# A sparse graph network on one core: the neighbour lists' numbers on ACT instead of GpSimd, and DVE's constants first

## The chip, the core and the metric

The kernel runs on one core of a Trainium2 chip. A core has five engines that run their own instruction streams and wait for each other through semaphores: PE (matrix multiply; PEld is its weight load), DVE (vector), ACT (activations), POOL (GpSimd) and SP, which here only issues DMAs. Sixteen DMA engines move data between HBM and the on-chip memory SBUF; PSUM holds matmul results. The metric is the time of one execution on the device in microseconds (us). Before the change the median of three runs is 1838.98 us (1837.8 to 1839.6).

## The reference: what is computed

Four graph layers over n = 4096 nodes with 256 features. Each normalises x, applies relu, and adds an attention over the neighbours that `adj` names; `adj` is a 4096 x 4096 matrix of int32, symmetric, with ones on the diagonal, and very sparse (about 0.2% ones).

```python
adj = bernoulli(0.000976562); adj = (adj | adj.T | eye).astype(int32)
h = max(layernorm(x), 0); x = x + L0(h, adj)   # four heads, leaky relu, softmax over neighbours, elu
h = max(layernorm(x), 0); x = x + L1(h, adj)   # one head, adds h @ W as well
h = max(layernorm(x), 0); x = x + L2(adj, h)   # four heads with biases
h = max(layernorm(x), 0); x = x + L3(h, adj)   # q, k, v attention, masked by adj.T
# L0, per head:
Wh = (h @ W);  e_ij = leaky_relu(s_i + s_j, 0.2) where adj_ij else -inf
out = elu(softmax_j(e) @ Wh)
```

## The kernel before, in words

A row below means 128 nodes, one to a partition; there are `nt` = 32 of them. The kernel has two parts. The **scan** (`scan`, 0 to about 430 us) reads the 64 MB of `adj` once and turns each node's row of it into a list of at most 24 neighbour numbers. The **layers** (`layers`) then never touch `adj`: for each place of the lists they gather neighbours' table rows with indirect DMAs from POOL (line 755) and weigh them. A dense version exists for inputs that the lists cannot hold; it does not run on these inputs.

*One row in the scan.* SP loads a row of `adj` in four quarters (`load`, L250, eight buffers); ACT casts each quarter to fp8 (`cast`, L261). In `marks`, PE makes from 512 columns a PSUM tile in which a neighbour stands as MARK plus its distance from the end (L476 with `mark`, L481 with the constants `stands` and `places`), and DVE takes the largest 8 of each 256 columns (MAX8, L483). After eight such steps `merge` picks the row's largest 24 into `s_top` (L491, L493). `number` turns these into table indices in `self.ids`, a part of the tile `s_keep`: POOL clips them to [MARK, MARK + n] (L500) and writes MARK + n minus that as uint32 (L503). An empty place becomes n, the number of a filler row.

*Layer 0 starts inside the scan.* During the first 36 steps `table` makes layer 0's table (ACT L325, L336, L341; PE L333, L748), which SP stores to HBM (L384). `early(j)` then serves rows 2j and 2j + 1: POOL fetches the table rows of six neighbours each, 12 indirect DMAs (L755, tile `s_g`, three buffers), DVE, ACT, PE and again ACT weigh and sum them (L523 to L560). `sort` ranks all nodes by their number of neighbours; its result `s_pos` (L639) says where each node goes. `to_place(t)` sends row t there with an indirect DMA from POOL (L645, `s_placed`). When all 32 sends have landed, `reload` reads the rows back in their new order and the layers begin.

*What sets the order.* PE, DVE, ACT and SP run in program order. The program is written as a loop over steps: `at` counts them, four to half a row (`t = at // 4`, `halves` = 64), so row r is marked in steps 8r to 8r + 7 and merged in the last of these. `plan` puts further work of an engine at a step, and at each step ACT's comes first, then PE's, the marks, the merge, DVE's and POOL's, and last the sends. POOL is not in the list of hand-ordered engines: its order is chosen by the framework's scheduler from when it takes things to be ready; only numbers and fetches keep their order among themselves (`in_turn`), and a send stays behind the last fetch written before it. In the kernel before, the number of row r is planned on POOL at 8(r + 1). A pair j has its fetches at `begin` = max(4(10 + j), 4(4j + 4)); its first DVE work stands at `last`, which is at least 17 steps later and 13 after the pair before; its ACT copy comes 20 steps after `last`. Sends are allowed from t = 59 on, except at t = 60 and t = 64, at most 12 of them before t = 64:

```python
if t > halves - 6 and t not in (halves - 4, halves):
    upto = min(placed + (2 if s % 2 else 1), 12 if t < halves else nt)
```

*The start.* SP brings x in eight groups of four rows (`bring`, L272). Before the loop, DVE computes statistics of groups 0, 1 and 2 (L569, L570), ACT and DVE make their scales (`norms_of`, L575 to L585), and DVE sums layer 0's weights (L166, L169). DVE's part of the constants (`constants`, L424 to L453) comes after group 0 and the weights. The class defines `constants` twice; the later definition is the one that is called, so the first hunk of the diff below is in a function that never runs.

Of the kernel before, what the change touches and what calls it, by code (L numbers as in the profile page):

```python
# [9 lines left out]
F32 = mybir.dt.float32  # L10
# [3 lines left out]
AF = mybir.ActivationFunctionType  # L14
ALU = mybir.AluOpType
# [4 lines left out]
P = 128  # L20
# [17 lines left out]
TOPK = 24  # L38
# [6 lines left out]
MARK = 8192.0  # L45
# [24 lines left out]
class Sparse:  # L70
# [30 lines left out]
    def constants(self):  # L101
        nc, const = self.nc, self.const
        self.ident = const.tile([P, P], F32, name="s_ident")
        make_identity(nc, self.ident)
        self.ident_bf = const.tile([P, P], BF16, name="s_ident_bf")
        nc.vector.tensor_copy(self.ident_bf, self.ident)
        self.mark = const.tile([P, P], BF16, name="s_mark")
        nc.vector.tensor_scalar(self.mark, self.ident, MARK, None, ALU.mult)

        self.below = const.tile([P, P], BF16, name="s_below")  # L110
        ones = self.ones = const.tile([P, P], BF16, name="s_ones")
        nc.vector.memset(ones, 1.0)
        nc.vector.memset(self.below, -1.0)
        nc.gpsimd.affine_select(
            out=self.below, in_=self.below, pattern=[[-1, P]], compare_op=ALU.is_ge, fill=0.0,
            base=0, channel_multiplier=1,
        )
        self.eps = const.tile([P, 1], F32, name="s_eps")
        nc.vector.memset(self.eps, EPS)

    def load_w(self, name, w):
        w_sb = self.const.tile([P, KC, D], F32, name=f"s_w_{name}")
        if len(w.shape) == 3:
            for c in range(KC):
                self.nc.sync.dma_start(
                    out=w_sb[:, c, :].rearrange("p (h f) -> p h f", h=4),
                    in_=w[:, ts(c, P), :].rearrange("h p f -> p h f"),
                )
        else:
            self.nc.sync.dma_start(out=w_sb, in_=w.rearrange("(c p) f -> p c f", p=P))  # L130
        return w_sb
# [105 lines left out]
    def scan(self, w0, a0):  # L237
# [3 lines left out]
        nc, nt, n = self.nc, self.nt, self.n  # L241
        halves, groups = 2 * nt, nt // 4
# [3 lines left out]
        def load(upto):  # L246
            while state["load"] < min(upto, 4 * nt):
                q = state["load"]
                raw[q] = self.pool.tile([P, n // 4], I32, name=f"s_raw_{q}", tag="raw", bufs=RAW)
                nc.sync.dma_start(  # L250
                    out=raw[q], in_=self.adj[ts(q // 4, P), ts(q % 4, n // 4)]
                )
                state["load"] += 1

        def cast(upto):
            while state["cast"] < min(upto, 4 * nt):
                q = state["cast"]
                r, h = divmod(q, 4)
                if h == 0:
                    low[r] = self.pool.tile([P, n], F8, name=f"s_low_{r}", tag="low", bufs=5)  # L260
                nc.scalar.activation(  # L261
                    low[r][:, ts(h, n // 4)], raw.pop(q), AF.Copy, saturate=False,
                    accum_out=self.sums[:, r, h : h + 1],
                )
                state["cast"] += 1
# [2 lines left out]
        make_identity(nc, self.ident)  # L268
        self.eps = self.const.tile([P, 1], F32, name="s_eps")
        nc.vector.memset(self.eps, EPS)  # L270
        xl = lambda g: self.keep[:, 4 * g : 4 * (g + 1), 0:D]
        bring = lambda g: nc.sync.dma_start(  # L272
            out=xl(g),
# [2 lines left out]
        norms, scale = {}, {}  # L276

        def stats(g, k):
            if k == 0:
                norms[g] = self.norms_of(self.pool, xl(g), 4, f"t{g}")  # L280
            next(norms[g])

        def scaled(g):
            scale[g] = next(norms[g])

        bring(0)
        first = self.extended("l0", w0, a0, 4)
# [3 lines left out]
        bring(1)  # L291
        load(RAW - 2)
        bring(2)
        for k in range(4):
            stats(0, k)
        next(norms[0])
        scaled(0)
        *_, (self.we0, _) = first
        cast(2)
        self.constants()  # L300
        for g in range(1, 3):
            for k in range(4):
                stats(g, k)
            next(norms[g])
            scaled(g)
            cast(2 * g + 2)
        later = self.weights()
        next(later)

# [2 lines left out]
        def plan(engine, at, *work):  # L312
            todo[engine].setdefault(at, []).extend(work)

        def run(engine, at):
            for work in todo[engine].pop(at, ()):
                work()
# [31 lines left out]
        for g in range(3, groups):  # L349
            begin = 4 * (g - 3)  # L350
# [2 lines left out]
            plan("act", begin + 6, lambda g=g: next(norms[g]))  # L353
            plan("dve", begin + 8, lambda g=g: scaled(g))
        for r in range(nt):
            plan("pool", 8 * (r + 1), lambda r=r: self.number(r))
        whole, last = [], 0
        for j in range(nt // 2):
            begin = max(4 * (10 + j), 4 * (4 * j + 4))
            stages = self.early(j)  # L360
            step = lambda stages=stages: next(stages)
            plan("pool", begin, step)

            last = max(last + 13 if j else begin + 24, begin + 17)
            plan("dve", last, step)
            for k in range(3):
                plan("dve", last + 2 + k, step)
            for k in range(EARLY + 1):
                plan("pe", last + 6 + 2 * k, step)
            plan("act", last + 2 * EARLY + 8, step)  # L370
            whole.append(last + 2 * EARLY + 8)
# [6 lines left out]
        for at in range(end + 1):  # L378
            t, s = divmod(at, 4)
            r, half = divmod(t, 2)  # L380
            if s == 0:
                g = t - 3
                if 0 <= g < groups:
                    nc.sync.dma_start(  # L384
                        out=self.tab[0][4 * g * P : 4 * (g + 1) * P, :].rearrange(
                            "(t p) w -> p t w", p=P
                        ),
                        in_=self.keep[:, 4 * g : 4 * (g + 1), D : D + W],
                    )
                if t + 3 < groups:  # L390
                    bring(t + 3)
                if 2 <= t < 7:
                    next(later, None)
            if s in (0, 2):
                load(state["cast"] + RAW)
                cast(2 * t + 4 + min(10, max(0, t - 8)) + s // 2 + 1)
            run("act", at)
            run("pe", at)
            if t < halves:
                if s == 0 and half == 0:  # L400
                    cand = self.pool.tile(
                        [P, n // CH, 8], F32, name=f"s_cand_{r}", tag="cand", bufs=2
                    )
                self.marks(r, 4 * half + s, low[r], cand)
                if s == 3 and half == 1:
                    self.merge(r, cand)
            run("dve", at)
            run("pool", at)
            if t > halves - 6 and t not in (halves - 4, halves):

                upto = min(placed + (2 if s % 2 else 1), 12 if t < halves else nt)
                while placed < upto and whole[placed // 2] < at:
                    self.to_place(placed)
                    placed += 1
# [80 lines left out]
    def number(self, r):  # L495

        nc, n = self.nc, self.n
        ids = self.pool.tile([P, TOPK - 1], F32, name=f"s_ids_{r}", tag="ids")
        self.in_turn(
            nc.gpsimd.tensor_scalar(ids, self.top[:, r, 1:], MARK, MARK + n, ALU.max, ALU.min)  # L500
        )
        self.in_turn(
            nc.gpsimd.tensor_scalar(  # L503
                self.ids[:, r, 0 : TOPK - 1], ids, -1.0, MARK + n, ALU.mult, ALU.add
            )
        )

    def early(self, j):
# [1167 lines left out]
```

## Time and profile before

| | |
|---|---|
| median of 3 runs | 1838.98 us (1837.8 to 1839.6) |
| the profiled execution | 1841.32 us |
| its span, first to last instruction | 1839.6 us |
| granted PE clock, mean | 0.751 |
| DVE busy | 1379.9 us, 75% |
| POOL busy | 1184.8 us, 64% |
| PE busy | 994.8 us, 54% |
| ACT busy | 423.7 us, 23% |
| number, L500 and L503 | 32 of each on POOL, median 298 and 229 ns |
| fetch or send on POOL, L755 and L645 | about 0.95 and 0.97 us each, 0.30 between two |
| last merge of the scan ends | 380.76 us |
| last send of the scan ends | 427.77 us |
| first fetch of the layers | 432.29 us |

A timeline line gives the start, the duration, the engine, the line of the kernel, the operation, the tiles that it writes and reads, and in brackets how long the engine was idle before it and what ended that. A count (x4) means that several instructions are merged. A share of busy time is a mean over stages with different limits, so each stage has to be read by itself.

### The profile page before, as it was taken

The numbers are of one execution on the slowest core, as the hardware profiler recorded it, in microseconds if no ns is written. First come the engines' busy times: TensorE is split into PE (matmuls) and PEld (weight loads), VectorE is DVE, ScalarE is ACT, GpSimd is POOL, SyncE is SP. The second block draws the span as 40 slices with busy tenths as digits, with TensorE's granted clock in tenths as the row PEclk, the third lists the DMA queues.
The fourth block names the chain that finished last, engine by engine and source line by source line (L and its number), as shares of the span: only waits on it lengthen the run. The fifth ranks groups of instructions, "written<-read, shape, count | busy, mean of one in ns | idle before, by whom it ended". The sixth has DMA issues, their size and how long they took to land. (4 is left out here: it accounts for less than half of the span.)

```text
span 1839.6 us, 14362 instructions
## 1 busy us (share of the span) xinstructions
PE 994.8 (54%) x2569; PEld 481.7 (26%) x2569; DVE 1379.9 (75%) x3900; ACT 423.7 (23%) x1240; POOL 1184.8 (64%) x1324
## 2 busy tenths in 40 slices
PE   4878787750666611222232167788785344565555
PEld 3523232220455400111111023343342111221122
DVE  6899989850688808888888257888885587887777
ACT  5864435000244401111111002222222000000000
POOL 1067756676566357777776477777772577776774
PEclk9988889875788855555555588889987676777777
DMA  9899877348533134444444344444443577666763
GB/s 319 281 394 363 287 259 254 97 148 242 168 87 88 51 84 128 131 132 130 132 132 121 69 111 133 134 135 131 136 131 97 156 215 210 208 208 181 209 205 108
DMA packets 123017, 312.89 MB, mean 170 GB/s; under 512 B 31236, under 2 KB 49671, under 8 KB 122920
## 3 DMA queue, kind: packets, MB, share of 16 engines
q0 software_dynamic: 68064, 207.46, 39.7%
q1 hardware_dynamic: 54856, 104.44, 16.2%
q14 instruction: 73, 0.60, 0.1%
q8 instruction: 24, 0.39, 0.1%
HBM read 276.80 MB, written 35.00 MB: 169 GB/s over the span
## 5 line engine op out<-in xcount | busy, mean ns | idle before, releaser
L755 POOL DMA_INDIRECT s_ring<-s_tab,s_near x924 | 883.8, 956 | 356.7 <-issue 190.4
L1033 PE MATMUL s_acc<-s_ring,s_ident 128*128 128x512 f32 x588 | 319.5, 697 | 183.3 <-issue 95.0
L1033 PEld LDWEIGHTS s_acc<-s_ring,s_ident 128*128 128x128 f32 x588 | 130.5, 228 | 368.2 <-issue 245.5
L755 POOL DMA_INDIRECT s_g<-s_tab,s_keep x192 | 183.2, 954 | 64.3 <-issue 57.0
L483 DVE MAX8 s_cand<-s_pt 128x8 f32<-128x256 f32 x512 | 181.6, 417 | 16.4 <-PE s_pt L481 15.9
L1028 DVE TENSOR_TENSOR s_ring<-s_ring,s_shares 128x2048 f32<-128x2048 f32 (+7 forms) x121 | 187.5, 1573 | 0.0
L740 PE MATMUL s_pht<-s_ident,s_h 128*128 128x128 f32 x128 | 34.3, 361 | 248.0 <-ACT s_h L732 248.0
L748 PE MATMUL s_ps<-s_we_l,s_ht 128*128 128x264 f32 x256 | 113.4, 586 | 79.2 <-ACT s_ht L742 79.2
L999 DVE SCALAR_TENSOR_TENSOR s_acc<-s_ring,s_p,s_acc 128x256 f32<-128x256 f32 x277 | 135.7, 490 | 9.7
L261 ACT ACTIVATE s_low<-s_raw 128x1024 fp8e4<-128x1024 int32 x128 | 134.2, 1050 | 21.3 <-DMA s_raw<-in_adj_dram 18.1
L556 PE MATMUL s_ae<-s_g,s_ident 128*128 128x512 f32 x192 | 113.7, 688 | 36.5 <-DVE s_g L547 36.5
L913 DVE TENSOR_TENSOR s_e<-s_ring,s_rx 128x8 f32<-128x8 f32 (+12 forms) x87 | 15.7, 181 | 148.0 <-DMA s_ring<-s_tab,s_near 143.0
L476 PE MATMUL s_pt<-s_low,s_mark 128*128 128x512 fp8e4 x256 | 107.7, 421 | 34.3 <-DVE s_cand L483 15.0
L748 PE MATMUL s_ps_kv<-s_wkv,s_ht 128*128 128x512 f32 x128 | 82.9, 782 | 73.6 <-ACT s_ht L742 73.6
L932 DVE TENSOR_TENSOR s_ring<-s_ring,s_shares 128x2048 f32<-128x2048 f32 (+7 forms) x48 | 81.1, 1690 | 47.8 <-DMA s_ring<-s_tab,s_near 31.5
L481 PE MATMUL s_pt<-s_places,s_stands 128*128 128x512 bf16 x256 | 106.5, 416 | 1.4 <-DVE s_stands L453 1.4
L952 ACT ACTIVATE s_shares<-s_e 128x32 f32<-128x32 f32 (+8 forms) x87 | 17.4, 200 | 387.8 <-DVE s_e L945 340.2
L575 ACT ACTIVATE s_y<-s_mv,s_eps 128x1 f32<-128x1 f32 x96 | 28.3, 294 | 294.0 <-DVE s_mv L570 294.0
L740 PEld LDWEIGHTS s_pht<-s_ident,s_h 128*128 128x128 f32 x128 | 18.3, 172 | 287.9 <-ACT s_h L732 271.9
L748 PEld LDWEIGHTS s_ps<-s_we_l,s_ht 128*128 128x128 f32 x256 | 63.0, 272 | 110.0 <-ACT s_ht L742 100.1
L935 DVE TENSOR_REDUCE s_e<-s_ring 128x32 f32<-128x2048 f32 (+7 forms) x48 | 81.2, 1692 | 1.7
L1021 PE MATMUL s_acc<-s_me,s_ident 128*128 128x512 f32 x60 | 42.8, 803 | 70.8 <-DVE s_me L1014 67.2
(193 smaller groups left out, 1673.4 us busy)
## 6 DMA issues: line engine op xcount, KB each, us to landing
s_raw<-in_adj_dram SPq DMA_DIRECT2D x128, 512.0 KB, 7.8
s_ring<-s_tab,s_near POOLq DMA_INDIRECT x924, 3.0
s_rx<-s_placed SPq DMA_DIRECT2D x32, 262.0 KB, 8.0
s_tab<-s_kv SPq DMA_DIRECT2D x32, 256.0 KB, 2.8
s_tab<-s_keep SPq DMA_DIRECT2D x8, 528.0 KB, 6.8
s_tab<-s_rx SPq DMA_DIRECT2D x32, 132.0 KB, 2.3
s_keep<-in_x_dram SPq DMA_DIRECT2D x8, 512.0 KB, 4.1
s_vself<-s_tab SPq DMA_DIRECT2D x32, 128.0 KB, 2.9
```

Of the source, the lines that this page charges most:

```text
L261: nc.scalar.activation(low[r][:, ts(h, n // 4)], raw.pop(q), AF.Copy, saturate=False, accum_out=self.sums[:, r, h : h + 1],)
L476: nc.tensor.matmul(pt, lhsT=self.mark, rhs=lo[:, ts(g, IB)], start=True, stop=False)
L481: nc.tensor.matmul(pt, lhsT=self.stands[:, g, :], rhs=self.places, start=False, stop=True)
L483: nc.vector.max(out=cand[:, g * (IB // CH) + k, :], in_=pt[:, ts(k, CH)])
L556: nc.tensor.matmul(acc, lhsT=self.ident, rhs=g[:, :, k, 0:D], start=False, stop=(k == E - 1))
L748: self.nc.tensor.matmul(ps[:, :width], lhsT=ht[:, c, :], rhs=w[:, c, :], start=(c == 0), stop=(c == KC - 1),)
L755: return self.nc.gpsimd.indirect_dma_start(out=out, out_offset=None, in_=table[:, :], in_offset=bass.IndirectOffsetOnAxis(ap=idx, axis=0),)
L932: nc.vector.tensor_tensor(kq, kq, q.unsqueeze(1).to_broadcast([P, m, D]), ALU.mult)
L935: nc.vector.tensor_reduce(e[:, k0 : k0 + m, :], kq.rearrange("p k (h d) -> p k h d", h=4), AX.X, ALU.add)
L999: nc.vector.scalar_tensor_tensor(acc, g[:, k, 0:D], p[:, k, :], acc, ALU.mult, ALU.add)
L1028: nc.vector.tensor_tensor(v, v, p[:, k0 : k0 + m, :].unsqueeze(3).to_broadcast([P, m, H, D // H]), ALU.mult)
L1033: nc.tensor.matmul(both, lhsT=self.ident, rhs=g[:, k : k + 2, v0 : v0 + D], start=(k == 0 and not full), stop=(k + 2 >= K),)
```

## The change

Four edits:

- `number` runs on ACT: two Relu activations, each with a bias per partition. The first takes MARK away (negative results become 0), the second computes relu(n - a). The values are the same as before. It is planned at step 8(r + 1) + 2 on ACT instead of 8(r + 1) on POOL. The two biases are new constants, filled by DVE memsets.
- `begin` of a pair's fetches is 16(j + 1) + 3 instead of 16(j + 1) where this term is the larger; its later stages follow.
- Sends are held back in the four steps from 256 on only; those of t = 60 are no longer held.
- At the start `self.constants()` comes ahead of all statistics; group 0 joins the loop of the other two.

```diff
@@ scan
+        self.over = self.const.tile([P, 1], F32, name="s_over_mark")
+        nc.vector.memset(self.over, -MARK)
+        self.none = self.const.tile([P, 1], F32, name="s_none_n")
+        nc.vector.memset(self.none, float(n))
...
-        for k in range(4):
-            stats(0, k)
-        next(norms[0])
-        scaled(0)
-        *_, (self.we0, _) = first
-        cast(2)
         self.constants()
-        for g in range(1, 3):
+        for g in range(3):
             for k in range(4):
                 stats(g, k)
             next(norms[g])
             scaled(g)
             cast(2 * g + 2)
+            if g == 0:
+                *_, (self.we0, _) = first
...
-            plan("pool", 8 * (r + 1), lambda r=r: self.number(r))
+            plan("act", 8 * (r + 1) + 2, lambda r=r: self.number(r))
...
-            begin = max(4 * (10 + j), 4 * (4 * j + 4))
+            begin = max(4 * (10 + j), 16 * (j + 1) + 3)
...
-            if t > halves - 6 and t not in (halves - 4, halves):
+            if t > halves - 6 and not nt // 2 * 16 <= at < nt // 2 * 16 + 4:
@@ number
-        ids = self.pool.tile([P, TOPK - 1], F32, name=f"s_ids_{r}", tag="ids")
-        self.in_turn(
-            nc.gpsimd.tensor_scalar(ids, self.top[:, r, 1:], MARK, MARK + n, ALU.max, ALU.min)
-        )
-        self.in_turn(
-            nc.gpsimd.tensor_scalar(
-                self.ids[:, r, 0 : TOPK - 1], ids, -1.0, MARK + n, ALU.mult, ALU.add
-            )
+        a = self.pool.tile([P, TOPK - 1], F32, name=f"s_ids_{r}", tag="ids")
+        nc.scalar.activation(a, self.top[:, r, 1:], AF.Relu, bias=self.over)
+        nc.scalar.activation(
+            self.ids[:, r, 0 : TOPK - 1], a, AF.Relu, bias=self.none, scale=-1.0
         )
```

The first hunk of the full diff adds the same two tiles to the unused definition of `constants`.

More of the change, by code (lines that the diff above doesn't have):

```diff
@@ L270, in scan @@
         nc.vector.memset(self.eps, EPS)
+        self.over = self.const.tile([P, 1], F32, name="s_over_mark")
+        nc.vector.memset(self.over, -MARK)
+        self.none = self.const.tile([P, 1], F32, name="s_none_n")
+        nc.vector.memset(self.none, float(n))
         xl = lambda g: self.keep[:, 4 * g : 4 * (g + 1), 0:D]
```

## The prediction

> **What bounds the kernel now.** First the clock and span of the one core (1839.6 us, clock 0.751), then the windows of the scan and the hand-over to the layers, because every edit lies before 430 us. The page's chain of work that ended last accounts for some 1% of the span, so I follow the end of the scan by hand. The windows (window, its length, then busy us and instructions of PE, PEld, DVE, ACT, POOL; clock; DMA share; GB/s):
>
> ```profile
> 50.00:100.00 50.00, 43.42 (x200) 26.38 (x199) 45.12 (x160) 44.50 (x99) 5.37 (x11) 0.97 0.90 290
> 300.00:350.00 50.00, 34.16 (x101) 13.38 (x102) 44.65 (x119) 13.40 (x28) 31.22 (x39) 0.85 0.48 158
> 350.00:400.00 50.00, 33.01 (x88) 12.32 (x86) 34.98 (x101) 1.47 (x4) 35.48 (x43) 0.84 0.38 125
> 400.00:450.00 50.00, 9.37 (x14) 3.49 (x14) 8.79 (x21) 1.32 (x3) 35.04 (x37) 0.57 0.71 233
> ```
>
> DVE sets the pace of the scan (45 of 50 us), with ACT as full beside it only up to 100 us, where it also makes layer 0's table. From 350 on DVE empties and POOL does not: its 35 us are descriptors at 0.95 us, each followed by 0.30 us that the trace calls issue, so it is full. The timeline of POOL and DVE there (start, us, engine, line, [idle before]):
>
> ```profile
> 361.66 0.30 POOL L500 TENSOR_SCALAR s_ids<-s_top 128x23 f32<-128x23 f32 x1 [2.35 <-DVE s_top L491]
> ...
> 376.66 0.95 POOL L755 DMA_INDIRECT s_g<-s_tab,s_keep  x1 [0.30 <-issue]
> 377.91 0.99 POOL L645 DMA_INDIRECT s_placed<-s_keep,s_pos  x1 [0.30 <-issue]
> ...
> 380.47 0.29 DVE L491 MAX8 s_top<-s_cand 128x8 f32<-128x128 f32 x1
> ...
> 384.28 0.96 POOL L645 DMA_INDIRECT s_placed<-s_keep,s_pos  x1 [0.30 <-issue]
> 385.28 0.34 POOL L500 TENSOR_SCALAR s_ids<-s_top 128x23 f32<-128x23 f32 x1
> 385.69 0.23 POOL L503 TENSOR_SCALAR s_keep<-s_ids 128x23 uint32<-128x23 f32 x1
> 385.90 0.29 POOL L500 TENSOR_SCALAR s_ids<-s_top 128x23 f32<-128x23 f32 x1
> 386.27 0.23 POOL L503 TENSOR_SCALAR s_keep<-s_ids 128x23 uint32<-128x23 f32 x1
> 386.99 1.08 POOL L755 DMA_INDIRECT s_g<-s_tab,s_keep  x1 [0.49 <-issue]
> ...
> 426.80 0.97 POOL L645 DMA_INDIRECT s_placed<-s_keep,s_pos  x1 [0.30 <-issue]
> 430.36 0.16 POOL L711 IOTA s_place_of<- 128x32 f32 x1 [2.59 <-DMA s_placed<-s_keep,s_pos]
> ```
>
> The last row's list is ready on DVE at 380.76, but its fetches begin at 386.99: POOL is sending six rows away (377.91 to 385.24), then makes four number instructions. After 386.99 it goes without a gap through 12 fetches and 20 sends to 427.77; the layers' first fetch follows at 432.29. So the end of this stage is the start of the last 12 fetches plus 40.8 us.
>
> At the start DVE waits for x and then for ACT:
>
> ```profile
> 14.54 0.61 PE L481 MATMUL s_pt<-s_places,s_stands 128*128 128x512 bf16 x1 [1.39 <-DVE s_stands L453]
> 15.65 0.43 DVE L569 BATCH_NORM_STATS2 s_st_t<-s_keep 128x6 f32<-128x256 f32 x1 [1.16 <-DMA s_keep<-in_x_dram]
> 27.91 0.16 DVE L582 SCALAR_TENSOR_TENSOR s_rn_t<-s_y_t 128x4 f32<-128x4 f32 x1 [5.05 <-ACT s_h_t L325]
> ```
>
> **What the Trainium skill says.** "ScalarE: Activation LUTs", section "Table sets: the hidden batching unit", says that relu is in every table set. The trace agrees: one table load in the whole scan, though L325 runs Relu 32 times. "DMA: Bandwidth & Descriptors", section "SWDGE vs HWDGE vs iDMA", says that a GpSimd core computes the descriptors of POOL's DMAs in software; the trace agrees in that each holds POOL for 0.95 us, so a number instruction and a descriptor compete for one engine.
>
> **The change, part by part.**
>
> *Numbers from POOL to ACT.* Leaves POOL: 64 instructions. In the tail the two pairs plus the longer gap cost 386.99 − (385.24 + 0.30) = 1.45 us. Comes to ACT: 64 Relu with a bias per partition. No such shape is in the trace; "ScalarE: Activation LUTs", section "What ACT_TABLE_LOAD costs", prices one at 280 + 0.833·23 = 299 ns (an estimate); the trace's bias-carrying L575 takes 298 ns for 4 columns and its plain L577 206. I take 0.30 for each, 0.33 from the first to the dependent second (as L575 to L577), so a pair is done 0.63 us after it starts and occupies ACT for about 0.54, since the next one overlaps by 0.09. Bounds of the pair: 0.41 (two of L577) to 0.70.
>
> *Where ACT would wait or be late.* ACT takes work in program order, so behind a waiting number stand casts, table stages and the exponentials. A number comes three planned steps after its merge. In the table stage (steps 0 to 36) there are four, at steps 10, 18, 26, 34. Each stands behind a known ACT instruction: row 0 at about 42.1 (merge ended 40.55), row 1 at 59.8 (58.69), row 2 at 73.5 (73.27), row 3 at 83.9 (83.29). None waits; each costs its 0.54. Row 0 is absorbed in ACT's own 1.80 us idle before L325 at 46.04. Row 1 delays a PSUM release that PE waits for (1.72 us at 60.13), so DVE loses about 0.4. Row 2 falls in a stretch of ACT without idle and costs 0.5. Row 3 falls before idles of 0.38 and 0.51. Sum: +0.8 us on DVE, from 0 to 4 × 0.54 = 2.2. After step 36 the planned casts lead by 8 to 14 quarters, which DVE uses at 7.05 / 4 = 1.76 us each, so 14 us cover ACT's holds of at most 3 us; without the cover each hold would cost DVE its length. POOL's fetches between 96 and 240 close up from 16.5 to 15.0 us per pair of rows, but DVE waits for none of them there except the first (3.2 us at 116.63), which starts on a store's landing, not on a number: 0.
>
> *Later early stages, `begin`.* From pair 10 on, DVE's, PE's and ACT's part comes 2 to 3 steps later. DVE's wait of 0.8 us for a fetch (300 to 350) goes: −0.8, from −0.8 to 0. Pair 12 now starts at step 228, around the sort at 229: about 0.9 + 2 × 1.7 us of DVE work falls after the sort, so the places come some 4 us earlier, near 347 instead of 351.07. The work before each merge is the same, so merges 29 and 31 stay at about 361.6 and 380.8.
>
> *Sends in t = 60.* Four of the six later sends now come ahead of pair 14's fetches, two behind. POOL then does 10 sends × 1.28 from 351.36 at the latest = 364.2, 12 fetches = 15.2 → 379.4, two sends → 381.9; with places at 347 it starts at 348.2 (pair 13's fetches end at 347.9), waits for row 29 until about 362.3, and is free at 380.1. What is late next is row 31: merge 380.76 + 0.10 (DVE to ACT, as L531 to L535) + 0.63 + 0.29 (to POOL, as from the places) = 381.8. Both bounds meet near 381.8, so the last fetches start 386.99 − 381.8 = 5.2 us earlier. ACT is free then: its last work before, the exponentials of pair 13, was done at 364. Pair 15's copy (417.58 before) also moves up, and row 30's send comes 8 us later: covered. End of the table: −5.2, from −1.45 (only the four instructions go) to −6.
>
> *Constants first.* The 2.45 us of DVE work between 12.03 and 14.48 move to about 1.9 to 5, where DVE was idle 3.96 us waiting for x; two memsets of 0.06 us join. But the next work on DVE starts on x's second load at 15.65, so the idle there only grows from 1.16 to 3.6, and the first MAX8 (28.19) still waits for ACT. L481's earlier start helps nobody. SP issues the same DMAs in the same order. 0, from −2.45 to +0.3 (constants still running when x lands at 4.92).
>
> *Sum:* −5.2 + 0.8 − 0.8 + 0 = −5.2 us. The profiled execution took 1841.3 us (span 1839.6 and 1.7 around it), 2.3 above the median shown, so 1836.1 for such an execution and 1838.98 − 5.2 = 1833.8 for the median. All later work waits for the placed rows, so the shift should arrive whole.
>
> **Rivals.**
> - *POOL's order stays*: its order is made by a scheduler from estimated readiness; if six sends still stand between the last two sets of fetches, or the pair on ACT is late, only 1.45 us go: 1837.5. For it: the sends were moved ahead of earlier-emitted numbers at 351 to 359. Against: sends emitted first have so far gone first when ready.
> - *The start is worth its 2.45 us*: the row loop starts earlier by all the moved DVE work: 1831.3. For it: PE's first wait for DVE, 12.4 us. Against: x's landing at 15.65.
> - *ACT becomes the pacer (slower)*: each number holds the ACT queue between 28 and 150 us, where ACT is 60 to 90% busy. If all twelve rows there pay 0.54 us plus about 0.6 of hold for a merge that comes later than ACT, DVE loses 14 us and the end is 1838.98 + 14 − 6 = 1847. It decides from a loss of 8.9 us on (5.2 + 3.7), eight of those rows. Against: the four arrival times above and the lead of casts.
>
> **How the numbers follow.** 0.2% is 3.7 us, about what this measurement can tell from no change. The forecast (5.2, own range 1832 to 1835.3) gets 0.64, POOL's order 0.18, the start 0.09, ACT 0.07, nothing of these 0.02, laid on no change. Faster: 0.64 + 0.09 = 0.73; within 0.2%: 0.18 + 0.02 = 0.20; slower 0.07. The range reaches from the start's case, 1830.5 with a half us of spread, to the case of POOL's order with its spread of one, 1838.5; what is left out is mostly the slower rival.
>
> **What would show it.** Right: no TENSOR_SCALAR on POOL after 5 us; two Relu of about 0.3 us on ACT per row; row 31's pair near 381.5 and the last 12 fetches about 1.0 us after the last merge; ten sends before pair 14's fetches; the layers' first fetch near 427. Right at the start: first MAX8 still near 28.2 and a longer wait for x. Wrong if the merge of row 31 moves by more than 2 us either way, if sends stand between row 31's numbers and its fetches, or if ACT shows waits for s_top followed by PE waiting for ACT.

## The result, and the profile after

The changed kernel takes 1827.67 us (median of 4 runs, 1827.12 to 1829.74); the kernel before takes 1839.29 beside it (1837.8 to 1840.61). The ratio is 0.9941, with a 95% interval of 0.9927 to 0.9955, so 11.6 us are gone and not 5.2. The forecast had the sign right and the time 6 us too long: 1827.67 lies below its range (1830.5 to 1838.5).

The profiled executions tell where it went. Before: 1841.32 us, span 1839.6. After: 1827.61 us, span 1825.9, granted clock 0.752. The difference of the spans, 13.7 us, has two parts. The layers' first fetch starts at 425.28 and not 432.29 (7.0 us). Their last starts at 1795.29 and not 1810.40 (15.1 us), so another 8.1 us were gained between the first and the last fetch of a part whose program was not touched; 1.4 of these are lost again behind the last fetch.

First the end of the scan in the changed kernel, from its timeline (start, us, engine, line, [idle before it and what ended that]):

```profile
376.60 1.00 POOL L645 DMA_INDIRECT s_placed<-s_keep,s_pos  x1 [0.30 <-issue]
377.90 0.99 POOL L645 DMA_INDIRECT s_placed<-s_keep,s_pos  x1 [0.30 <-issue]
379.20 0.99 POOL L755 DMA_INDIRECT s_g<-s_tab,s_keep  x1 [0.30 <-issue]
...
383.52 1.42 DVE L487 MAX8 s_cand<-s_pt 128x8 f32<-128x256 f32 x4 [1.75 <-PE s_pt L485]
...
385.51 0.95 POOL L755 DMA_INDIRECT s_g<-s_tab,s_keep  x1 [0.30 <-issue]
386.41 0.29 DVE L495 MAX8 s_top<-s_cand 128x8 f32<-128x128 f32 x1
386.74 0.31 ACT L503 ACTIVATE s_ids<-s_top,s_over_mark 128x23 f32<-128x23 f32 x1 [12.89 <-DVE s_top L495]
387.08 0.31 ACT L504 ACTIVATE s_keep<-s_ids,s_none_n 128x23 uint32<-128x23 f32 x1
387.67 0.94 POOL L755 DMA_INDIRECT s_g<-s_tab,s_keep  x1 [1.21 <-ACT s_keep L504]
...
419.76 0.97 POOL L645 DMA_INDIRECT s_placed<-s_keep,s_pos  x1 [0.31 <-issue]
423.32 0.16 POOL L711 IOTA s_place_of<- 128x32 f32 x1 [2.60 <-DMA s_placed<-s_keep,s_pos]
```

Row 31's merge now ends at 386.70, 5.9 us *later* than before (380.76). All the same the stage ends earlier, because the twelve fetches of the last pair no longer stand together behind it. Six of them, row 30's, run from 379.20 on, while DVE is still at row 31; POOL then rests 1.21 us for row 31's number, makes the other six, and ends its sends at 420.73 instead of 427.77. From the last merge to the layers' first fetch it was 51.5 us; it is 38.6.

The windows of the same stretch (busy us and instructions of PE, PEld, DVE, ACT, POOL; clock; DMA share; GB/s): DVE and ACT work longer before 400 us, POOL as fully as before.

```profile
350.00:400.00 50.00, 38.04 (x91) 14.44 (x91) 39.35 (x106) 4.74 (x14) 37.45 (x39) 0.80 0.46 150
400.00:450.00 50.00, 7.57 (x14) 2.77 (x12) 6.23 (x15) 0.63 (x2) 34.95 (x38) 0.61 0.78 241
```

At the start (the timeline of DVE) x's second load and the wait for ACT come 0.8 us sooner than the 15.65 and 27.91 of before; the first MAX8 starts at 27.39, before 28.19.

```profile
14.89 0.43 DVE L569 BATCH_NORM_STATS2 s_st_t<-s_keep 128x6 f32<-128x256 f32 x1 [1.50 <-DMA s_keep<-in_x_dram]
27.11 0.16 DVE L582 SCALAR_TENSOR_TENSOR s_rn_t<-s_y_t 128x4 f32<-128x4 f32 x1 [5.05 <-ACT s_h_t L329]
```

Then the layers. The view of one tile gives an operation's durations as min/median/max in ns. The fetches of the layers (`s_ring`) in the kernel before:

```profile
L755 POOL DMA_INDIRECT s_ring<-s_tab,s_near x924: 949/953/1187, 432.3 to 1810.4; - x185
```

and in the changed kernel:

```profile
L755 POOL DMA_INDIRECT s_ring<-s_tab,s_near x924: 942/946/1127, 425.3 to 1795.3; - x185
```

Each fetch is 7 ns shorter. From one start to the next of fetches that follow each other directly (called their step below) it is 1.2573 us before and 1.2500 after (means over the timeline), 7.3 ns; 924 of them make 6.7 us, about what the layers gained. Added up, POOL's busy time in these fetches fell from 883.8 to 876.6 us. In the kernel before the step is no constant: up to 377 us its fetches are 1.250 us apart too, and from row 30's and 31's numbers on 1.257.

### The profile page after: what moved, and what is told of

It is laid out like the page before. It is cut to its first block, busy times and chain, and to the rows that moved or that the text cites. A ratio compares the mean times of both kernels' runs of the same rounds, so it can differ in the third digit from the quotient of the medians.

```text
span 1825.9 us, 14363 instructions
## 1 busy us (share of the span) xinstructions
PE 993.0 (54%) x2569; PEld 480.8 (26%) x2569; DVE 1380.7 (76%) x3902; ACT 441.8 (24%) x1304; POOL 1159.2 (63%) x1260
## 5 line engine op out<-in xcount | busy, mean ns | idle before, releaser
L755 POOL DMA_INDIRECT s_ring<-s_tab,s_near x924 | 876.6, 949 | 357.7 <-issue 190.3
L748 PE MATMUL s_ps_kv<-s_wkv,s_ht 128*128 128x512 f32 x128 | 79.0, 750 | 71.6 <-ACT s_ht L742 71.6
```

The source lines that it names most:

```text
L748: self.nc.tensor.matmul(ps[:, :width], lhsT=ht[:, c, :], rhs=w[:, c, :], start=(c == 0), stop=(c == KC - 1),)
L755: return self.nc.gpsimd.indirect_dma_start(out=out, out_offset=None, in_=table[:, :], in_offset=bass.IndirectOffsetOnAxis(ap=idx, axis=0),)
```

## The experiments

Two kinds of chip came up. On the first, that of the result above, the kernel before takes 1838 to 1840 us (medians); on the second, met on three chips, 2174 to 2195. The granted clock of the profiled executions is 0.747 to 0.755 on the first and 0.712 to 0.718 on the second. A time of the second kind is compared only with its like.

### One part of the change at a time

`e1`: the kernel before, unaltered.

> The kernel before, unchanged, profiled once more beside the others. Two numbers of its first trace are to be repeated or not: the pace of POOL's back-to-back fetches in the layers (1.2573 us from one to the next between 650 and 950 us, against 1.2500 after the change), and the start of the layers' first fetch (432.3 us). If the slower pace belongs to the program before, it comes again, 1.257. If it belongs to one execution or one chip, this trace shows 1.250, or the changed kernels of this call show 1.257 too. Time: 1839 us within 2.

Measured: 1839.72 (1836.79 to 1843.25), ratio 1.0005 [0.9996, 1.0014]; the fetches of the layers are 1.2575 to 1.2593 us apart between 650 and 950 us. So the longer step is no accident of one execution.

`e2`: the numbers alone go to ACT, with their two bias tiles and two steps earlier than in the change; sends, `begin` and the start as before.

```diff
-            plan("pool", 8 * (r + 1), lambda r=r: self.number(r))
+            plan("act", 8 * (r + 1), lambda r=r: self.number(r))
...
```

> Only the numbers go to ACT (planned at step 8(r + 1), with the two bias tiles); fetches, sends and start as before. Six sends still stand ahead of pair 15's fetches, so the prediction's arithmetic gives only the 1.45 us of the four POOL instructions at the end of the scan: first fetch of the layers near 430.8. Theory N (the layers' pace comes from number instructions in POOL's stream): pace 1.250 us in the layers, 6 us more, about 1832. Theory T (from the two added tiles, which move what lies behind them): also 1.250. Theory S (from where sends and fetches stand): 1.257, about 1837.5.

Measured: 1832.17 (1830.03 to 1833.31), ratio 0.9964 [0.995, 0.9978], so 6.3 us under the 1838.47 beside it. None of it is in the scan: the layers' first fetch starts at 432.09. The fetches are 1.250 us apart to the end, and it is 1368.0 us from the first of the layers to the last, against 1376.5 in `e1`. In the scan ACT now waits for merges. Its waits from 20 to 130 us (us in total, times, longest):

```profile
ACT s_ids L503 <- DVE s_top L495: 8.6, 5, 4.3
```

Behind these numbers stand casts and copies, and so DVE waits 6.8 us for row matmuls in that stretch, against 2.7 before; row 3's merge comes 3.7 us later than in the kernel before, the last four 4.7 to 5.5.

`e3`: the constants alone come first on DVE.

```diff
+        self.constants()
...
-        for g in range(1, 3):
+        for g in range(3):
...
```

> Only the constants go first; no new tile, numbers on POOL. Prediction: 0, the first MAX8 stays at 28.2 us. If the change's 0.8 us earlier first MAX8 (27.39) is this edit's, it comes here too: 27.4, and the time is 0.8 us less. Pace in the layers 1.257 by theories N, T and S; 1.250 only if DVE's or PE's early order had a part in it.

Measured: 1839.01 (1831.86 to 1842.94), ratio 0.9996 [0.9986, 1.0007]. The first MAX8 comes at 27.53, 0.7 us sooner, and the end of the scan hardly moves (431.67). In `e2`, whose constants are where they were, it comes at 27.31, so the start's 0.8 us is not this edit's own; and kernels with one and the same start have it anywhere from 27.08 (`e15`) to 27.67 (`e16`) on this kind of chip. What gives it is open; it doesn't show in the whole.

`e4`: the changed kernel with the numbers back on POOL; its sends, its `begin`, its constants and its two tiles stay.

```diff
-            plan("act", 8 * (r + 1) + 2, lambda r=r: self.number(r))
+            plan("pool", 8 * (r + 1), lambda r=r: self.number(r))
...
```

> The changed kernel with the numbers back on POOL (two instructions per row, step 8(r + 1)); the two tiles, the constants first, the later begin and the freed sends stay. Theory N: pace 1.257 in the layers. Theory T: 1.250. Theory S: 1.250. End of the scan: two sends, then four number instructions, then twelve fetches that start only after the numbers of row 31, so if the gain of 7 us at the end of the scan rests on row 30's fetches not waiting for row 31, it is lost here but for the earlier sends: first fetch of the layers 428 to 431.

Measured: 1838.99 (1837.49 to 1841.6), ratio 1.0006 [0.9998, 1.0015]: without the numbers on ACT the rest of the change is worth nothing. The fetches are 1.258 us apart. Row 31's merge ends at 386.25, as late as in the changed kernel, and all twelve fetches begin behind it at 387.5. The lateness of that merge thus isn't ACT's doing. `e15` below has the old sends and the same late merge, and `e3` has neither the new `begin` nor the late merge (381.04); what is left is `begin`, three steps later, or the tiles, which nothing links to it. That it is `begin` is thus shown by elimination, not by a run of its own. The waits of DVE from 345 to 388 us in the changed kernel name the engine; before, DVE waited 0.2 us for the same.

```profile
DVE s_cand L487 <- PE s_pt L485: 4.2, 4, 1.8
```

In PE's order the sums of an early pair (`s_ae`) stand between the last rows' matmuls in both kernels. In the kernel before, pair 13's come ahead of row 30's merge, and two of them take about 1 us:

```profile
370.65 1.12 PE L556 MATMUL s_ae<-s_g,s_ident 128*128 128x512 f32 x2 [2.61 <-DVE s_g L547]
```

In the changed kernel DVE makes these products only behind row 30's merge. PE stands 4.43 us at the sums, with the rest of row 31's matmuls behind them, and then two sums take 1.9 to 2.1 us and a row matmul 0.63 (0.38 before):

```profile
377.18 2.08 PE L556 MATMUL s_ae<-s_g,s_ident 128*128 128x512 f32 x2 [4.43 <-DVE s_g L547]
379.05 0.63 PE L480 MATMUL s_pt<-s_low,s_mark 128*128 128x512 fp8e4 x1
```

The granted clock from 377.1 to 383.3 us is 0.50, and 1.00 from 370.6 to 378 in the kernel before; that the pause is the reason isn't shown. Pair 12's sums hold up row 29 in the same way at 356.32.

### What makes the fetches 7 ns longer

`e5` moves only the numbers of rows 30 and 31 to ACT, in the kernel before; `e6` leaves only these two on POOL, in the changed kernel.

```diff
+            plan("act" if r >= 30 else "pool", 8 * (r + 1), lambda r=r: self.number(r))   # e5
+            plan("act" if r < 30 else "pool", 8 * (r + 1) + (2 if r < 30 else 0), lambda r=r: self.number(r))   # e6
...
```

> The kernel before with the numbers of rows 30 and 31 alone on ACT; the numbers of rows 0 to 29 stay on GpSimd. In the kernels whose numbers are on GpSimd the period of back-to-back fetches goes from 1.250 to 1.257 us just behind the numbers of rows 30 and 31. Theory A (these last two pairs, standing behind sends, set the pace of all fetches after them): here 1.250 us from 388 us to the end, and the layers 6 to 7 us shorter than in the kernel before (last fetch less first 1368 to 1370 us, where before has 1378). Theory B (it is the number of GpSimd instructions or its 64 number operations as a whole): 1.257 us stays, 1375 to 1378 us.

> The changed kernel with the numbers of rows 30 and 31 alone back on GpSimd, each in its turn ahead of the twelve fetches of pair 15. Theory A: the period of the fetches behind them is 1.257 us, and last fetch less first in the layers 1375 to 1378 us. Theory B: 1.250 us and 1370 us. On the scan's end both say: all twelve fetches start behind row 31's merge and its number, so the first fetch of the layers comes 5 to 8 us later than the changed kernel's 425.3.

Both met a chip of the slower kind (2188.94 and 2207.86, one run each, beside a median of 2194.78 for the kernel before), but the step of the fetches can be read there too: 1.260 us in the layers of both, from 1.252 and 1.254 early in the scan. `e5` speaks against theory A, `e6` against theory B: neither the last two rows nor all 64 operations are needed. In `e6` the last twelve fetches begin at 452.53, together, behind row 31's number, as both theories said; how much that costs isn't told, as the changed kernel wasn't run on this chip.

Next, instructions without meaning in the numbers' places. `e9` is the changed kernel itself, for comparison. `e10` adds two memsets of a spare tile for each row; `e11` a single pair of TENSOR_SCALARs in the first microseconds; `e13` two TENSOR_SCALARs for each row, unread; `e17` the same for rows 0 to 27 alone, which all run ahead of the first send.

```diff
+            plan("pool", 8 * (r + 1), self.idle)      # e10, e13; e17 only for r < 28
+    def idle(self):
+        for _ in range(2):                            # e10
+            self.in_turn(self.nc.gpsimd.memset(self.spare, 1.0))
...
+        self.in_turn(self.nc.gpsimd.tensor_scalar(    # e13, e17; e11 once, in constants
+            self.spare, self.ident[:, : TOPK - 1], 0.0, 1.0, ALU.max, ALU.min))
+        self.in_turn(self.nc.gpsimd.tensor_scalar(self.whole, self.spare, -1.0, 2.0, ALU.mult, ALU.add))
```

> The changed kernel itself, unaltered, on whichever chip this call gets: 1827 to 1829 us where the kernel before takes 1839; back-to-back fetches 1.250 us apart, before as after 388 us. If the pace were a matter of the chip or of one execution, it would be 1.257 here.

> The changed kernel with two GpSimd memsets of a spare tile (128x23) for every row, where the kernel before has its two number operations: as many GpSimd instructions as before, at the same places, with nothing behind them. Theory L (the fetches' pace comes from how many or where instructions stand in GpSimd's stream): 1.257 us in the layers, some 6 us lost against the changed kernel. Theory K (it comes from the kind of work: elementwise TENSOR_SCALAR in a stream that also has sends): 1.250 us, and the time within 2 us of the changed kernel's.

> The changed kernel with a single pair of TENSOR_SCALARs of a number's form on GpSimd, on spare tiles in the first microseconds, 100 us ahead of the first fetch; nothing reads them. Theory L: as two instructions shift the stream by little, either pace, but not linked to the kind. Theory K in its strong form (once such an operation has run, all fetches behind the sends are slow): 1.257 us in the layers and 5 to 7 us lost. Theory K in its weak form (the operation has to stand between fetches or behind sends): 1.250 us and nothing lost.

> The changed kernel with two GpSimd TENSOR_SCALARs of the numbers' form and size for every row, at the places of the kernel before, on spare tiles that nothing reads; the real numbers stay on ACT. Theory K (that kind of work between the fetches and the sends makes later fetches slow): 1.257 to 1.260 us in the layers. Theory R (it matters that the fetches read what GpSimd has written, or wait for it): 1.250 to 1.253 us.

> The same unread TENSOR_SCALARs on GpSimd as in e13, but for rows 0 to 27 alone, so that all stand ahead of the first send; from there on fetches and sends alone. If the slow pace needs them among or behind the sends: 1.250 us before and after 350 us, last fetch less first of the layers 1370 us. If it is enough that they ran between fetches: 1.2605 us from the first sends on, 1374 to 1377 us.

The fetches of the layers in the view of their tile; `e10`:

```profile
L761 POOL DMA_INDIRECT s_ring<-s_tab,s_near x924: 940/946/1177, 485.3 to 2137.0; - x185
```

`e13`:

```profile
L768 POOL DMA_INDIRECT s_ring<-s_tab,s_near x924: 951/957/1210, 427.4 to 1801.9; - x185
```

`e17`:

```profile
L769 POOL DMA_INDIRECT s_ring<-s_tab,s_near x924: 940/946/1167, 484.3 to 2144.8; - x185
```

Their steps are 1.2500 (`e10`), 1.2500 (`e11`), 1.2605 (`e13`) and 1.2500 us (`e17`); `e9` has 1.253, but in it, as in `e7`, the fetches early in the scan already have it. So as many POOL instructions as before do nothing when they are memsets, and an early pair of TENSOR_SCALARs does nothing either. (`e10` took 2178.49 us, ratio 1.0023 [1.0005, 1.0041], `e11` 2177.53, ratio 1.0002 [0.9983, 1.002], where `e9` has 2178.45 and 1.0010.) Unread TENSOR_SCALARs among the fetches and sends bring the longer step back in full, from the first sends on. Of the same TENSOR_SCALARs, those ahead of the first send do nothing. On a chip of the first kind `e13` took 1832.86 (one run, the kernel before 1838.99), with 1374.5 us from first to last fetch where the changed kernel has 1370.0.

What is shown: whether the step grows within a run goes with this kind of operation. In the seven traces that have TENSOR_SCALARs on POOL behind the first send (the kernel before, `e1`, `e3` to `e6`, `e13`) the layers' step is 5 to 11 ns longer than that of the fetches before 300 us; in the thirteen without them it is at most 2 ns longer (means, the layers' from 650 to 950 us). `e13` adds them and `e2` takes them away, both on the first kind of chip; the slower kind shows the growth too (`e5`, `e6`). It then stays for all 924 later fetches, though no such operation runs any more. From first to last fetch of the layers the first kind of chip has 1374.1 to 1378.1 us in the five traces with the longer step and 1368.0 to 1371.5 in the five without; the means are 6.2 us apart, and a single pair of traces, like the 8.1 us above, tells this only to some 4 us.

Why it grows is open, and "TENSOR_SCALARs behind sends" is not a sufficient rule. In the kernel before, pair 14's fetches, with numbers and sends mixed ahead of them, still have 1.251 us; in `e5`, behind the same order of numbers and sends, they have 1.261. In `e4` the step is 1.259 for pair 14's first fetches and about 1.248 for the last six, just behind row 29's number, and 1.256 again from 387.5 on. `e17` against `e13` is one execution each, on different kinds of chip.

### What brings the scan's end nearer

`e7`, `e12` and `e14` are one kernel: the changed one with the odd row's six fetches first in each pair, so that none of pair 15's can start without row 31's number.

```diff
-        for u in range(2):
+        for u in (1, 0):
             for k in range(E):
                 self.fetched = self.in_turn(
```

> The changed kernel with the two loops' order turned: of every pair's twelve fetches the six of the odd row come first. Theory (what the scan's end gains is that the six fetches of row 30 no longer stand behind row 31's number): none of pair 15's fetches can start before row 31's number, so GpSimd stands from about 379 to 387.7 us, and the layers' first fetch moves from 425.3 to 432 to 433; the pace in the layers stays 1.250; in all 1834 to 1836. Rival (the gain came from the sends' new places or from the later stages): under 2 us lost.

> The changed kernel with the six fetches of the odd row first in every pair, again, on a chip beside the changed kernel itself. Theory (row 30's six fetches, ahead of row 31's number, are what the scan's end gains): GpSimd stands from about 379 to 387.7 us, the layers' first fetch moves from 425.3 to 432 to 433, and the whole from 1828 to 1834 to 1836. Rival (the gain came from the sends' places or the stages' times): under 2 us lost.

> The changed kernel with the odd row's six fetches first in every pair. On a chip where the kernel before takes 1839 us. Theory (row 30's six fetches ahead of row 31's number are what the scan's end gains): GpSimd stands from about 379 to 387.7 us, the layers' first fetch at 432 to 433 and not 425.3, 1834 to 1836 in all. If, as on the slower chip, row 31's merge comes 6 us sooner with this order: 427 to 428, and 1830.

`e14` met a chip of the first kind: 1834.69 (1830.81 to 1839.91), ratio 0.9975 [0.9967, 0.9984], by the medians 7 us above the changed kernel. Its timeline:

```profile
381.62 0.99 POOL L645 DMA_INDIRECT s_placed<-s_keep,s_pos  x1 [0.31 <-issue]
387.67 0.99 POOL L755 DMA_INDIRECT s_g<-s_tab,s_keep  x1 [5.06 <-ACT s_keep L504]
```

Row 31's merge ends at 386.70, as in the changed kernel; POOL rests 5.06 us for its number instead of 1.21, and then has twelve fetches to make and not six. The layers' first fetch starts at 433.20, 7.9 us later. The step of the fetches stays 1.250. With this order the scan's whole gain is gone (432.29 in the kernel before) and the layers' stays. On the slower chips the same edit told nothing clear. `e12` was 2178.36 beside 2178.45 for `e9`, with the layers' first fetch 2.1 us later and not 7: row 31's six fetches start at 442.29 in place of 448.63, so its number was there some 6 us sooner with this order. Why is open; the theory's numbers missed there. Kernels with an unchanged order differ as much on that chip (`e10` 485.31, `e9` 487.29, `e11` 487.50). `e7` had 2207.87, ratio 1.0053 [1.0027, 1.0079], without the changed kernel beside it.

`e15` is the changed kernel with the old condition for the sends.

```diff
-            if t > halves - 6 and not nt // 2 * 16 <= at < nt // 2 * 16 + 4:
+            if t > halves - 6 and t not in (halves - 4, halves):
```

> The changed kernel with the old condition for the sends (none in t = 60, none in t = 64). Theory (each send ahead of pair 14's fetches fills time in which GpSimd waits for row 28's number): six sends and not ten before pair 14, GpSimd rests 5 us there, the layers' first fetch at 429 to 430.5 and not 425.3, 1831 to 1833 in all. Rival (those fetches start as soon as the six sends are done): under 1.5 us lost.

Measured: 1829.99 (1828.12 to 1831.77), ratio 0.9944 [0.9922, 0.9966], the layers' first fetch at 427.25, 2.0 us later; the whole can't be told from the changed kernel's. The expected wait is at another place and shorter. Behind six sends pair 14's fetches start at 356.91 already, as row 28's number is there, and the wait comes between the two rows of the pair:

```profile
366.92 0.94 POOL L755 DMA_INDIRECT s_g<-s_tab,s_keep  x1 [2.76 <-ACT s_keep L504]
```

The six sends that are left then stand ahead of pair 15's twelve fetches and cover the wait for row 31. So by these traces the sends in t = 60 are worth 2 us, and the order of the fetches, once numbers no longer stand in POOL's queue, is worth 7.9. The kernel before has its first fetch at 432.29 and 433.56 in its two traces; beside these 1.3 us the 7.9 are clear and the 2 hardly.

`e8` and `e18` are one kernel: the changed one with each number in step 8(r + 1), two steps sooner.

> The changed kernel with each pair of Relus in quarter 8(r+1), right behind its merge in the order, and not two quarters later. In the run with the numbers alone ACT waited 8.6 us for the merges of the table stage, and DVE then 5.7 us more for matmuls. Theory (the two quarters are what keeps ACT from being the pacer): the same waits here, merges and s_pos 4 to 5 us later, and the layers' first fetch at 429 to 430; 1831 to 1833 in all. Rival (the earlier numbers cost nothing, as ACT has slack): within 1 us of the changed kernel.

> The changed kernel with each pair of Relus in quarter 8(r+1), not 8(r+1)+2. Theory (two quarters of distance keep ACT from waiting for the merges of the table stage, where its casts, turns and copies stand behind the number): ACT waits some 8 us for s_top up to 130 us, DVE 4 us more for matmuls there; s_pos at 352 and not 348.5, the layers' first fetch at 428 to 430, 1830 to 1832 in all. Rival (ACT has slack): within 1 us of 1827.7.

Both met the slower kind of chip: 2207.88, ratio 1.0064 [1.0047, 1.008], and 2182.28, ratio 1.0031 [1.0016, 1.0046]; the changed kernel had 1.0010 [0.999, 1.003] in `e9`. Up to 130 us ACT waits for merges, as in `e2`; in `e9` it has no such wait there. From `e18`:

```profile
ACT s_ids L503 <- DVE s_top L495: 11.3, 6, 3.9
```

Row 3's merge comes 3 us later than in `e9` (85.81 and 82.84 for the start of its last MAX8), the places 4.5 us (398.4 and 393.9), and the layers' first fetch 4.4 us (491.67 and 487.29). The waits and the delay of row 3 are the theory's, on chips of the other kind than it named. Its later times fit, but are not shown: `e18` and `e9` met different chips, and kernels with the numbers two steps later have the places anywhere from 392 (`e10`) to 397 (`e12`). So with the numbers two steps nearer ACT does hold DVE up in the table stage, and two steps of distance keep that away; what it costs in the whole isn't told.

### A kernel that the traces point to

In the changed kernel POOL rests 6.8 us for `s_pos` before its first send at 348.75, and behind it only the 1.21 us for row 31's number. `e16` lets the casts run ahead by two more, plans the sort four steps sooner and allows 16 sends ahead of t = 64.

```diff
-        counted = 4 * (halves - 7)
+        counted = 4 * (halves - 8)
-                cast(2 * t + 4 + min(10, max(0, t - 8)) + s // 2 + 1)
+                cast(2 * t + 4 + min(12, max(0, t - 8)) + s // 2 + 1)
-                upto = min(placed + (2 if s % 2 else 1), 12 if t < halves else nt)
+                upto = min(placed + (2 if s % 2 else 1), 16 if t < halves else nt)
```

> The changed kernel with the casts two quarters' worth further ahead, the counting stage of the sort four quarters (some 6 us) sooner, and up to 16 sends instead of 12 ahead of t = 64. If GpSimd's work behind s_pos is what sets the scan's end: first send at 343 and not 348.75, 12 to 16 sends ahead of pair 15's fetches, row 31's six fetches right behind row 30's without a wait, the layers' first fetch at 420 to 421.5 and not 425.3; 1822 to 1825 in all. If the merges set it: they stay at 373 and 387 and the first fetch gains 1 to 2 us at most.

Measured: 1823.98 (1822.34 to 1828.46), ratio 0.9919 [0.9895, 0.9943], by its median 3.7 us under the changed kernel; the two intervals against the kernel before overlap. Its timeline:

```profile
346.35 1.01 POOL L645 DMA_INDIRECT s_placed<-s_keep,s_pos  x1 [3.04 <-DVE s_pos L639]
...
368.00 0.94 POOL L755 DMA_INDIRECT s_g<-s_tab,s_keep  x1 [1.60 <-ACT s_keep L504]
...
383.19 0.99 POOL L755 DMA_INDIRECT s_g<-s_tab,s_keep  x1 [0.30 <-issue]
```

The first send came 2.4 us sooner and not the expected 6, the layers' first fetch 2.3 us (422.99), 1.5 us later than the latest expected. Sixteen sends stand ahead of pair 15's fetches, and row 31's number, whose merge ends at 388.08, is there when its fetches come up: the wait is gone. What is left of POOL's rest in the stretch is 3.0 us for `s_pos` and 1.6 for row 29.

### The slower chips

The changed kernel gains nothing there: 2178.45 in `e9`, the kernel before 2174.58, ratio 1.0010 [0.999, 1.003]. POOL is less often the one that is late: in `e9` it rests 614.8 us in all before fetches of the layers, against 357.7 in the changed kernel on the first kind (both with the 0.30 us between any two). And the time from first to last fetch doesn't follow the step: on one chip 1662.0 us with 1.250 (`e12`), 1651.7 with 1.250 (`e10`) and 1648.2 with 1.253 (`e9`); on another 1662.5 with 1.260 (`e5`) and 1670.0 with 1.250 (`e8`). In the scan DVE is busy 142 us of the 200 between 100 and 300 us, where it has 182 on the first kind. Why these chips are slower, and where the scan's 7 us go on them, is open.

## Why the prediction was wrong

**"All later work waits for the placed rows, so the shift should arrive whole."** This is the step that failed. The shift did arrive, but with 4.6 us on top by the medians (11.6 less the 7.0 of the scan) and 6.7 by the profiles. With the scan's 7.0 alone the time would have been about 1832, inside the range. The sum put the layers at nothing because their program is untouched, yet POOL's fetches there became 7 ns shorter each. `e2` shows it by itself (6.3 us, none of it in the scan), `e4` shows it gone when the numbers are back, and `e13` shows that unread TENSOR_SCALARs among the sends bring the longer step back in the changed kernel; why they do is open. The trace of before held a hint, 1.250 us between fetches ahead of 377 us and 1.257 behind 388; it would have said that the pace can differ, hardly that this change moves it.

**The last fetches (−5.2).** Right in what it named and wrong in how. It had all twelve fetches behind row 31's number, with the merge unmoved at 380.76, and so 381.8. In fact row 30's six need row 30's number alone (it put pair 14's twelve behind row 29 in the same way); in POOL's queue before, the two numbers stood together ahead of all twelve. And the merge moved by 5.9 us, a size that the prediction itself named as what would make it wrong. The first is worth 7.9 us (`e14`), the second takes its part back, and −7.0 came out for the whole scan. That this lies near −5.2 is luck: two errors of 7.9 and 5.9 us had opposite signs. The measured links from the merge on were close: 0.04 us to ACT (0.10 forecast), 0.65 for the pair (0.63), 0.28 to POOL (0.29).

**"Merges 29 and 31 stay."** Wrong: 361.57 became 364.34 and 380.76 became 386.70. The work on DVE before each merge had been counted, and that the moved part of pair 12's would be paid for by earlier places. The places did come earlier, though less: 348.48 from 351.07, forecast 347. And PE was left out: with the stages later, its sums for pairs 12 and 13 hold up the last rows' matmuls, and DVE waits 4.2 us for PE where it waited 0.2.

**DVE's wait for a fetch (−0.8).** It went, as forecast.

**Sends in t = 60.** The order came as described: ten ahead of pair 14's fetches, two behind. By the trace of `e15` this part is worth 2 us, hardly clear of the scatter.

**Numbers in the table stage (+0.8).** About right (the rows' own parts, 0.4 and 0.5, add up to 0.9). A Relu of 128x23 takes 0.31 us, close to the estimate of 0.30 from the Trainium skill's page "ScalarE: Activation LUTs" (section "What ACT_TABLE_LOAD costs"). The merges are 0.85 us sooner than before up to row 2 and 0.4 from row 3 on, so the numbers cost some 0.5 us there, and ACT waits for no merge. Without the two steps of distance it waits 8.6 to 11.3 us (`e2`, `e8`, `e18`).

**Constants first (0).** The time is right, the picture not quite: the first MAX8 is 0.8 us sooner, but so it is in `e2`, without this edit. And DVE's wait for x's second load is 1.50 us and not 3.6: the constants run until 6.37 us, past the landing of x at 4.92, since they wait for POOL (0.85 and 0.38 us) and take longer at this place (L446 1.19 us, and 0.54 before as L442).

**The rivals.** "POOL's order stays" did not occur: no send stands between row 31's number and its fetches. "The start is worth its 2.45 us" fell with `e3`. "ACT becomes the pacer" fell for the change; its waits come up in a kernel in which the numbers stand two steps nearer.

## What to carry to other kernels

An instruction that waits in an in-order queue holds back everything behind it, also what doesn't need its result: ask for each item behind it what that item alone needs, since taking the waiting instruction out of the queue can free the others by more than its own length (here 7.9 us against 1.45). An engine that issues a thousand like DMAs back to back turns 7 ns of each into 7 us, so its step is worth reading before and behind each stage, and an unchanged program is no proof of an unchanged pace. Put small dependent work on an idle engine with some distance behind its producer, or the engine's other work waits with it.

## What the runs showed of the hardware

POOL's indirect gather of 128 rows of 264 f32 was 946 to 949 ns (median of the 924 in the layers) in the thirteen traces without TENSOR_SCALARs behind the first send, and 953 to 957 in the seven with them; POOL's indirect sends kept about 0.97 us and 1.27 to 1.28 us from start to start in both. The first fetch behind a TENSOR_SCALAR takes 1.02 us (the very first of the scan 1.13 to 1.22), 1.05 to 1.09 where sends have run since the last fetch, and behind sends alone 0.98 to 1.00; in a run of fetches it is 0.95. On ACT a Relu with a bias per partition takes 0.31 us for 23 columns, with f32 or uint32 as the output, and a dependent second one starts 0.35 us after the first. Two kinds of chip differ by 18 to 19% on the same kernel, and an edit that is worth 0.6% on one is worth nothing that could be measured on the other.
